# Four PSUM banks for attention scores: given out in fixed turn instead of by the pool's estimate (pre-norm attention with a routed expert layer, one core)

## The chip, the core and the metric

The kernel runs on one core of a Trainium2 chip. The metric is the device time of one execution in microseconds; lower is better. The kernel before the change was run three times: 604.11, 605.59 and 605.93 us, median 605.59. A profile was taken of one further execution. It took 598.14 us, of which 596.4 us lie between its first and its last instruction (the span).

## What is computed

One transformer layer in float32 on x of shape 8 x 512 x 128: attention on the normalised input, added back, and then a mixture of experts on the normalised sum, added back.

```
q = (x @ Wq).reshape(b, t, H, HD)            # H = 16 heads of HD = 8
k = (x @ Wk).reshape(b, t, H, HD)
v = (x @ Wv).reshape(b, t, H, HD)
s = jnp.einsum('bqhd,bkhd->bhqk', q * scale, k)
s = jnp.where(causal[None, None], s, -jnp.inf)
p = jax.nn.softmax(s, axis=-1)
o = jnp.einsum('bhqk,bkhd->bqhd', p, v).reshape(b, t, H * HD)
...
probs = jax.nn.softmax(logits / TEMPERATURE, axis=-1)       # 8 experts
topk_probs, topk_idx = jax.lax.top_k(probs, TOPK)           # the best 2
hidden = jax.nn.relu(jnp.einsum('th,ehf->tef', x_flat, w1) + b1[None])
all_out = jnp.einsum('tef,efh->teh', hidden, w2) + b2[None]
y_flat = jnp.sum(gathered * topk_probs[:, :, None], axis=1)
...
x = x + _L0_attn_ref(_layernorm(x, axis=-1), ...)
x = x + _L0_ffn_ref(_layernorm(x, axis=-1), ...)
```

## The kernel before

The work goes sequence by sequence: 8 sequences (b), each with 4 groups (g) of 4 heads. Several generators run side by side while the program is traced. Each yields a time of its own making, and a small loop at the end of the function always lets the one with the lowest time go on. What comes out is one written order for PE, ACT, DVE and SP, which these four engines keep (`ORDERED`, L1346 to L1359). POOL isn't in that set; its instructions are placed by the framework, apart from those that are pinned.

For each head the scores are computed twice. The generator `shifts` (L557) computes the scores with queries on the partitions, the tiles called s, for the row maximum alone: PE writes a bank of 128 x 512 float32 with up to four matmuls (L597, L602), and DVE reduces it to the maximum (pm, L616). When a group is done, the maxima are negated, split in two bfloat16 parts, turned by PE (nmTp, L562), copied by ACT (nmT, L564) and written by POOL's DMA as two more rows of the queries (L570). The generator `attend` (L642) then computes the scores with keys on the partitions, the tiles called st, with the shift by the row maximum already in the product: PE writes a bank (L752, L757) and ACT takes the exp of it into SBUF (pt, L762). PE multiplies the result with the values (po, L673). `shifts` runs some half a sequence ahead of `attend`, so that in the written order one unit of s tiles and one unit of st tiles take turns. A unit has two banks or one; in a group there are 10 s tiles and 10 st tiles.

All these tiles come from one pool of four PSUM banks, `ps_sc` (L123). A tile is asked for with `ps_sc.tile(..., tag="sc")` at L591 for s and at L747 for st. A third place asks for them too, after attention: the expert tiles ph of L1244, 42 of them, read by ACT and DVE (L1258, L1260) into hT. In all 682 tiles go through the four banks: 320 s, 320 st, 42 ph. Which of the four banks a tile gets is settled when the program is built: the framework estimates when each bank comes free, and gives the tile the one that it expects first. On the chip there is no choice left: the first matmul of the tile waits, by semaphore, for the reader of the tile that had the same bank before.

Three more banks (`ps_mm`, L124) serve all other products and transposes, and one (`ps_o`, L125) collects the output of attention. The expert layer runs in the generator `experts` (L1047): tiles of 128 tokens are gathered by expert, turned (xgTp, L1210), multiplied with w1 (ph, L1251), passed through bias and ReLU (hT), multiplied with w2 (py, L1110), given their second bias (yo, L1114) and scattered by POOL (ys, L1148). Part of it runs beside attention, the rest after it. Indirect transfers of POOL (L1016, L1148) are tied to the last exp that was written before them (`in_order`, L256). The generator `sums` adds the two choices of each token to x (L1329) and stores the result.

Of the kernel before, what the change touches and what calls it, by code (L numbers as in the profile page):

```python
# [9 lines left out]
F32 = mybir.dt.float32  # L10
# [5 lines left out]
PSUM = bass.MemoryType.PSUM  # L16
DRAM = bass.MemoryType.DRAM

P = 128
# [7 lines left out]
def preln_attn_moe(ctx: ExitStack, tc: tile.TileContext, x, wq, wk, wv, wo, bo,  # L27
# [37 lines left out]
    B, T, D = x.shape  # L65
    E, _, F = w1.shape
# [38 lines left out]
    for k, b in ((0, 1), (0, 3), (0, 5), (0, 6), (1, 7)):  # L105
        n = GROUPS[k].index(b) + 1
# [13 lines left out]
    work = ctx.enter_context(tc.tile_pool(name="work", bufs=2))  # L120
    small = ctx.enter_context(tc.tile_pool(name="small", bufs=2))
    slots = ctx.enter_context(tc.tile_pool(name="slots", bufs=1, space=DRAM))
    ps_sc = ctx.enter_context(tc.tile_pool(name="ps_sc", bufs=4, space=PSUM))  # L123
    ps_mm = ctx.enter_context(tc.tile_pool(name="ps_mm", bufs=3, space=PSUM))  # L124
    ps_o = ctx.enter_context(tc.tile_pool(name="ps_o", bufs=1, space=PSUM))  # L125

# [129 lines left out]
    def in_order(ins):  # L256
        tc.keep_in_program_order(ins)
        if last_exp[0] is not None:
            tc.add_manual_dep(
                ins.ins, last_exp[0].ins.name,  # L260
                mybir.DependencyInfo(
                    mybir.DependencyClass.Sync, mybir.DependencyReason.DATA
                ),
                reason="indirect transfers keep the pace of attention",
            )

    def mm_tile(name):
        return ps_mm.tile([P, T], F32, tag="mm", name=name)
# [14 lines left out]
    for k in range(2):  # L283
        n = E * ROOM[k] + SPARE * P
# [272 lines left out]
    def shifts():  # L557
        late = []

        def transposed(b, g, nh):  # L560
            pt = mm_tile(f"nmTp_{b}_{g}").bitcast(BF16)
            nc.tensor.transpose(pt[:, :P], nh, ident_bf)  # L562
            nmT = small.tile([32, P], BF16, tag="nmT", name=f"nmT_{b}_{g}")
            nc.scalar.copy(nmT, pt[:32, :P])  # L564
            late.append(lambda: rows(b, g, nmT))

        def rows(b, g, nmT):

            for l in range(2):
                ins = nc.gpsimd.dma_start(  # L570
                    out=q2_buf[b % 2][KS + l : KS + l + 1, HG * g : HG * g + HG],
                    in_=nmT[16 * l : 16 * l + 16],
                )
                if b > 0:
                    tc.keep_in_program_order(ins)
            shifted.add((b, g, 2))

        for b in range(B):
            for g in range(G):
                t0 = b - LEAD + g / G + (0.1 if b == 0 < g else 0.0)  # L580
                yield t0
                assert b in packed
                q2, k2 = q2_buf[b % 2], k2_buf[b % 2]

                pm = pm_buf[g % 2].rearrange("p (n u) t k -> p u n (t k)", u=2)
                for pr in range(2):
                    n = 2 * g + pr
                    for i, unit in enumerate(S_UNITS):
                        yield t0 + (3 * pr + i) / 24
                        for v, bank in enumerate(unit):  # L590
                            ps = ps_sc.tile(  # L591
                                [P, T], F32, tag="sc", name=f"s_{b}_{n}_{i}_{v}"
                            )
                            for u, t, at in bank:
                                h, q = 2 * n + u, ts(t, P)
                                if t > 0:
                                    nc.tensor.matmul(  # L597
                                        ps[:, at : at + t * P], lhsT=q2[:KS, h, q],
                                        rhs=k2[:KS, h, : t * P],
                                        start=(at == 0), stop=True, skip_group_check=True,  # L600
                                    )
                                nc.tensor.matmul(  # L602
                                    ps[:, at + t * P : at + (t + 1) * P],
                                    lhsT=q2[:, h, q], rhs=k2[:, h, q],
                                    start=(at + t == 0), stop=True, skip_group_check=True,
                                )
                            blocks = ps.rearrange("p (a q) -> p a q", q=P)
                            if i == 0:
                                top, src = pm[:, v, pr, 12:13], ps
                            elif i == 1:  # L610
                                top, src = pm[:, v, pr, 3:7], blocks
                            else:
                                top, src = pm[:, :, pr, 8], ps.rearrange(
                                    "p (u k) -> p u k", u=2
                                )
                            nc.vector.tensor_reduce(top, src, AX.X, ALU.max)  # L616
                        if t0 + (3 * pr + i) / 24 < 0:
                            keep_warm(WARM[2], f"{g}_{pr}_{i}")
                        if late:
                            late.pop(0)()  # L620
                nm = small.tile([P, HG * NT], F32, tag="nm", name=f"nm_{b}_{g}")
                nc.vector.tensor_reduce(
                    nm, pm_buf[g % 2].rearrange("p h t k -> p (h t) k"), AX.X, ALU.max,
                    negate=True,
                )
                nh = nh_buf[g % 2]
                nm = nm.rearrange("p (h o a) -> p h o a", o=2, a=2)
                hi, lo = (
                    nh[:, ts(l, HG * NT)].rearrange("p (h a o) -> p h o a", a=2, o=2)
                    for l in range(2)  # L630
                )
                V.tensor_copy(hi, nm)
                V.tensor_tensor(lo, nm, hi, ALU.subtract)
                if b > 0:
                    late.append(lambda: None)
                late.append(lambda b=b, g=g, nh=nh: transposed(b, g, nh))
        while late:
            late.pop(0)()
            yield B - LEAD + 0.05


    def attend():  # L642
# [90 lines left out]
        for b in range(B):  # L733
            for g in range(G):
                yield b + g / G
                assert (b, g, 2) in shifted
                q2, k2 = q2_buf[b % 2], k2_buf[b % 2]
                for i, unit in enumerate(T_UNITS):
                    pts = []
                    for pr in range(2):  # L740
                        yield b + g / G + (2 * i + pr + 0.5) / 24
                        n = 2 * g + pr
                        pt = work.tile(
                            [P, 2, T], F32, tag="pt", name=f"pt_{b}_{n}_{i}", bufs=6
                        )
                        for v, bank in enumerate(unit):
                            ps = ps_sc.tile(  # L747
                                [P, T], F32, tag="sc", name=f"st_{b}_{n}_{i}_{v}"
                            )
                            for u, j, at in bank:  # L750
                                h, k = 2 * n + u, ts(j, P)
                                nc.tensor.matmul(  # L752
                                    ps[:, at : at + P], lhsT=k2[:, h, k], rhs=q2[:, h, k],
                                    start=(at == 0), stop=True, skip_group_check=True,
                                )
                                if j < NT - 1:
                                    nc.tensor.matmul(  # L757
                                        ps[:, at + P : at + T - j * P],
                                        lhsT=k2[:KO, h, k], rhs=q2[:KO, h, (j + 1) * P :],
                                        start=False, stop=True, skip_group_check=True,  # L760
                                    )
                            last_exp[0] = nc.scalar.activation(pt[:, v, :], ps, AF.Exp, scale=SCALE)  # L762
                        pts.append(pt)
                        go_on()
                    products.append(lambda b=b, g=g, pts=pts, unit=unit, i=i: product(
                        b, g, pts, unit, i == 0, i == 2))
                attended.add((b, g))
# [279 lines left out]
    def experts():  # L1047
# [192 lines left out]
        for n, (s, i) in enumerate(tiles):  # L1240
            first, m = quad(s, i)
            yield when(s, i + 1)
            if after(s, i):
                ph = ps_sc.tile([P, T], F32, tag="sc", name=f"ph_{s}_{i}")  # L1244
                hT = work.tile([P, 2, T], F32, tag="pt", name=f"hT_{s}_{i}", bufs=6)
                hT = hT[:, 0, :].rearrange("p (c t) -> p c t", c=FC)
            else:
                ph = mm_tile(f"ph_{s}_{i}")
                hT = work.tile([P, FC, P], F32, tag="hT", name=f"hT_{s}_{i}")
# [138 lines left out]
```

## Time and profile before

| | before |
|---|---|
| median of three runs | 605.59 us |
| profiled execution | 598.14 us |
| its span | 596.4 us |
| mean granted TensorE clock | 0.954 |
| PE matmul rows of the s tiles, first to last start | 25.7 to 428.7 us |
| PE matmul rows of the st tiles, first to last start | 44.9 to 462.5 us |
| exp of st (L762), 320 | 179.1 us busy, 600 ns mean |
| maximum of s (L616), 320 | 206.0 us busy, 682 ns mean |
| idle time of ACT before the exps | 128.1 us |
| idle time of DVE before the maxima | 36.4 us |

Engines are PE (matmul), PEld (its weight loads), DVE, ACT, POOL and SP. "L762 ACT ACTIVATE pt<-st" is line 762, an instruction of ACT that writes the tile pt and reads the tile st. A line such as "PE s L597 <- ACT pt L762: 12.8, 23, 2.4" in the list of waits says that PE's matmuls into s at line 597 were held up, with the engine idle, until an instruction of ACT at line 762 had ended: 12.8 us in total, 23 times, at most 2.4 us. A PE row's end is modelled, since matmuls overlap in the array.

### The profile page before, as it was taken

How to read it: one execution, taken by the hardware profiler on the slowest of the kernel's cores; microseconds unless marked ns; L12 is line 12 of the kernel's file. 1: busy time of each engine (PE TensorE's matmuls, PEld its weight loads, DVE VectorE, ACT ScalarE, POOL GpSimd, SP SyncE). 2: the span in 40 equal slices, each digit the busy share in tenths (PEclk: the TensorE clock that was granted, in tenths of full speed). 3: DMA queues.
4: the chain of work that ended last, by engine and by line, in shares of the span. 5: the costliest groups of instructions: out<-in, count | busy, mean ns of one | idle time of the engine just before them, and what ended most of it. 6: DMA issues, size and time to landing. Idle time of an engine off the chain costs nothing. (4 is left out here: it accounts for less than half of the span.)

```text
span 596.4 us, 14010 instructions
## 1 busy us (share of the span) xinstructions
PE 515.4 (86%) x4762; PEld 378.0 (63%) x4762; DVE 430.9 (72%) x1367; ACT 306.5 (51%) x673; POOL 220.2 (37%) x278
## 2 busy tenths in 40 slices
PE   6979999988888988888799999998899788879980
PEld 4745455545445565665566777766576687879970
DVE  7788778898778977978788877797753354323694
ACT  2646656665645566465447465654454233345530
POOL 4032202315514422533443336335335334654441
PEclk9888899999979999999799999999999788999995
DMA  2568198188199455406502784322344586668783
GB/s 57 160 133 186 28 226 210 38 214 215 27 208 181 125 142 127 124 19 179 149 30 67 180 202 120 89 64 73 87 116 114 181 248 185 192 184 246 243 293 110
DMA packets 68762, 86.07 MB, mean 144 GB/s; under 512 B 11540, under 2 KB 50748, under 8 KB 66652
## 3 DMA queue, kind: packets, MB, share of 16 engines
q1 hardware_dynamic: 61508, 74.87, 49.1%
q0 software_dynamic: 6592, 9.65, 5.0%
q8 instruction: 39, 0.64, 0.5%
q10 hardware_dynamic: 592, 0.66, 0.4%
q14 instruction: 31, 0.25, 0.2%
HBM read 61.34 MB, written 26.16 MB: 147 GB/s over the span
## 5 line engine op out<-in xcount | busy, mean ns | idle before, releaser
L762 ACT ACTIVATE pt<-st 128x512 f32<-128x512 f32 x320 | 179.1, 600 | 128.1 <-PE st L752 58.3
L616 DVE TENSOR_REDUCE pm<-s 128x1 f32<-128x512 f32 (+2 forms) x320 | 206.0, 682 | 36.4 <-PE s L602 30.3
L1148 POOL DMA_INDIRECT ys<-yo,to x78 | 76.1, 975 | 125.4 <-ACT pt L762 50.2
L597 PE MATMUL s<-k,q 72*128 72x384 bf16 (+2 forms) x384 | 93.9, 280 | 16.0 <-ACT pt L762 12.8
L752 PE MATMUL st<-q,k 128*128 128x128 bf16 x512 | 92.9, 222 | 14.8 <-ACT pt L762 6.4
L602 PE MATMUL s<-k,q 128*128 128x128 bf16 x512 | 94.3, 223 | 7.4 <-ACT pt L762 5.5
L757 PE MATMUL st<-q,k 74*128 74x256 bf16 (+2 forms) x384 | 93.9, 280 | 0.0
L673 PE MATMUL po<-pt,va 128*18 128x512 f32 (+3 forms) x1024 | 92.5, 445 | 0.5 <-ACT pt L762 0.3
L1110 PE MATMUL py<-w_sb,hT 128*128 x624 | 88.6, 286 | 4.2 <-DVE yo L1114 2.0
L1016 POOL DMA_INDIRECT xs<-xn_f,slot x64 | 63.2, 987 | 64.1 <-ACT pt L762 35.7
L1110 PEld LDWEIGHTS py<-w_sb,hT 128*128 128x128 f32 x624 | 79.5, 199 | 8.2 <-issue 3.6
L602 PEld LDWEIGHTS <-q 128*128 128x128 bf16 x512 | 51.0, 100 | 37.7 <-issue 34.8
L570 POOL DMA_DIRECT2D q<-nmT x64 | 33.7, 529 | 76.4 <-ACT nmT L564 71.1
L597 PEld LDWEIGHTS <-q 72*128 72x128 bf16 x384 | 37.8, 100 | 36.5 <-issue 29.7
L752 PEld LDWEIGHTS <-k 128*128 128x128 bf16 x512 | 51.6, 101 | 6.3 <-issue 2.4
L757 PEld LDWEIGHTS <-k 74*128 74x128 bf16 x384 | 37.7, 98 | 26.2 <-issue 20.8
L673 PEld LDWEIGHTS po<-pt,va 128*18 128x18 f32 x1024 | 23.1, 97 | 29.6 <-issue 22.7
L1251 PE MATMUL ph<-xgT,wt 128*128 128x128 f32 x288 | 41.0, 286 | 0.8 <-ACT pt L762 0.8
L1251 PEld LDWEIGHTS ph<-xgT,wt 128*128 128x128 f32 x288 | 35.8, 195 | 5.7 <-issue 2.4
L1258 ACT ACTIVATE hT<-ph,q 128x128 f32<-128x128 f32 x72 | 21.0, 368 | 27.9 <-PE ph L1251 11.7
L1258 ACT ACTIVATE hT<-ph,wt 128x128 f32<-128x128 f32 x72 | 20.6, 367 | 22.3 <-issue 10.9
L456 POOL TENSOR_TENSOR part<-rest,part 128x512 bf16<-128x512 f32 x14 | 16.2, 1162 | 41.6 <-issue 33.8
(172 smaller groups left out, 688.0 us busy)
## 6 DMA issues: line engine op xcount, KB each, us to landing
wt<-wrows SPq DMA_DIRECT2D x36, 322.0 KB
k<-kparts SPq DMA_DIRECT2D x42, 192.0 KB
q<-wrows SPq DMA_DIRECT2D x24, 322.0 KB
k<-wrows SPq DMA_DIRECT2D x18, 322.0 KB
q<-qparts SPq DMA_DIRECT2D x30, 192.0 KB
q<-ys SPq DMA_DIRECT2D x15, 256.0 KB
k<-xs SPq DMA_DIRECT2D x42, 65.0 KB
qparts<-part SPq DMA_DIRECT2D x14, 192.0 KB
```

The costliest lines, as they stand in the source:

```text
L597: nc.tensor.matmul(ps[:, at : at + t * P], lhsT=q2[:KS, h, q], rhs=k2[:KS, h, : t * P], start=(at == 0), stop=True, skip_group_check=True,)
L602: nc.tensor.matmul(ps[:, at + t * P : at + (t + 1) * P], lhsT=q2[:, h, q], rhs=k2[:, h, q], start=(at + t == 0), stop=True, skip_group_che ...
L616: nc.vector.tensor_reduce(top, src, AX.X, ALU.max)
L673: nc.tensor.matmul(po[32 * h : 32 * h + 2 * VC, j * P :], lhsT=va[:, j, c0 : c0 + 2 * VC], rhs=at_cols(pts[pr], unit, u, at, W), start=(fi ...
L752: nc.tensor.matmul(ps[:, at : at + P], lhsT=k2[:, h, k], rhs=q2[:, h, k], start=(at == 0), stop=True, skip_group_check=True,)
L757: nc.tensor.matmul(ps[:, at + P : at + T - j * P], lhsT=k2[:KO, h, k], rhs=q2[:KO, h, (j + 1) * P :], start=False, stop=True, skip_group_c ...
L762: last_exp[0] = nc.scalar.activation(pt[:, v, :], ps, AF.Exp, scale=SCALE)
L1016: ins = nc.gpsimd.indirect_dma_start(out=xs[k], out_offset=bass.IndirectOffsetOnAxis(ap=slot[b][:, j * NT + i : j * NT + i + 1], axis=0), ...
L1110: nc.tensor.matmul(py, lhsT=hT[:, c, :], rhs=w2_sb[:, bass.ds(at[s, i] + c * E * D, D)], start=(c == 0), stop=(c == FC - 1),)
L1148: ins = nc.gpsimd.indirect_dma_start(out=ys[k], out_offset=bass.IndirectOffsetOnAxis(ap=to[s, first][:, i - first : i - first + 1], axis=0 ...
L1251: nc.tensor.matmul(ph[:, ts(c, P)], lhsT=wt[s, i][:, ts(c, P)], rhs=turned[s, first][:, ts(i - first, P)], start=True, stop=True,)
L1258: nc.scalar.activation(hT[:, c, :], ph[:, ts(c, P)], AF.Relu, bias=bias)
```

## The change

The pool `ps_sc` gets four tags of one buffer each in place of one tag of four buffers. A counter in the new function `score_tile` walks over the four tags; all three places that asked the pool for a tile now ask `score_tile`. So the bank of a tile is that of the tile four before it in traced order. The number of banks, the instructions and the written order of PE, ACT, DVE and SP stay.

```
-    ps_sc = ctx.enter_context(tc.tile_pool(name="ps_sc", bufs=4, space=PSUM))
+    ps_sc = ctx.enter_context(tc.tile_pool(name="ps_sc", bufs=1, space=PSUM))
...
+    turn = [0]
+
+    def score_tile(name):
+        turn[0] = (turn[0] + 1) % 4
+        return ps_sc.tile([P, T], F32, tag=f"sc{turn[0]}", name=name)
...
-                            ps = ps_sc.tile(
-                                [P, T], F32, tag="sc", name=f"s_{b}_{n}_{i}_{v}"
-                            )
+                            ps = score_tile(f"s_{b}_{n}_{i}_{v}")
...
-                            ps = ps_sc.tile(
-                                [P, T], F32, tag="sc", name=f"st_{b}_{n}_{i}_{v}"
-                            )
+                            ps = score_tile(f"st_{b}_{n}_{i}_{v}")
...
-                ph = ps_sc.tile([P, T], F32, tag="sc", name=f"ph_{s}_{i}")
+                ph = score_tile(f"ph_{s}_{i}")
```

## The prediction

> **What bounds the kernel now.** I read the page's busy times first, then the chain of waits, the list of who waited for whom, the view of the tiles s and st, and last the timeline, stretch by stretch.
>
> ```profile
> span 596.4 us, 14010 instructions
> ...
> PE 515.4 (86%) x4762; PEld 378.0 (63%) x4762; DVE 430.9 (72%) x1367; ACT 306.5 (51%) x673; POOL 220.2 (37%) x278
> ```
>
> PE is the busiest engine, DVE second. The chain that ended last, by line:
>
> ```profile
> PE py L1110 7%; PE ph L1251 6%; DVE x L1329 1%; PE xgTp L1210 1%; DMA q<-ys 1%; ACT hT L1258 0%; DVE yo L1114 0%; DVE hT L1260 0%; DMA ys<-yo,to 0%; PE pp L725 0%; PE oqp L694 0%; PE oTp L717 0%; ACT xgT L1212 0%; PE pl L801 0%; POOL ys L1148 0%
> ```
>
> What carries time there are PE's expert matmuls after attention; attention ends with the last exp at 463 us, and from there a late PE is a late end. So what PE loses in attention is lost at the end.
>
> The list of waits shows what a full pool costs PE today:
>
> ```profile
> PE s L597 <- ACT pt L762: 12.8, 23, 2.4
> ...
> PE st L752 <- ACT pt L762: 6.4, 12, 1.0
> ...
> PE s L602 <- ACT pt L762: 5.5, 9, 1.6
> ...
> PE st L752 <- DVE pm L616: 3.3, 7, 1.0
> ```
>
> Columns: total us, times, longest. A matmul that opens a score tile waits for the reader of the bank's last tile, and that reader is mostly an exp. The reader of the other kind, the row maximum, is slower:
>
> ```profile
> L616 DVE TENSOR_REDUCE pm<-s x320: 656/680/694, 26.1 to 429.5; 128x1 f32<-128x512 f32 x64, 128x4 f32<-128x512 f32 x64, 128x2 f32<-128x512 f32 x32
> ```
>
> The exp's row has 570/597/656 ns. The gap in durations is small; the gap in queueing isn't. I put the 682 tiles of the pool in PE's order, gave each the bank that the compiled program of before has for it, its first matmul's start, and its reader's end. An s tile holds its bank 1.90 us on average from first matmul to release, an st tile 1.33; a reduce begins a median 0.61 us after its scores stand, an exp 0.17. The shortest time from a release to the next tile's first matmul is 0.050 us.
>
> **The change part by part.** It adds no instruction and removes none; PE, ACT, DVE and SP keep their written order. It changes which reader a tile's first matmul waits for: always that of the tile four before. Today that holds for 265 of the 678 tiles that follow another; 413 reuse a bank 1, 2, 3, 5, 6 or 7 tiles old. The first 31 tiles and all 42 ph tiles (L1251) have distance four already; the closest ph tile finds its bank free 3.1 us before it, so they cost nothing.
>
> *What it removes.* 81 tiles start after a gap of over 0.1 us that a bank's release ended, 33.9 us in all: 28.0 behind an exp, 5.9 behind a reduce. At 75 tiles that wait for their bank at distance other than four, the bank four back was free sooner; the part of the gap that goes is 14.1 us.
>
> *What it adds.* For 80 tiles, the reader four back ended later than the tile began: 37.5 us, of which 36.7 behind reduces. Neither sum is the price, because PE is one queue: once late, it finds the following banks free. One stretch shows it:
>
> ```profile
> 250.00 0.32 PE L597 MATMUL s<-k,q 72*128 72x384 bf16 x1 [0.43 <-ACT pt L762]
> ...
> 250.49 0.22 PE L752 MATMUL st<-q,k 128*128 128x128 bf16 x1
> ...
> 250.56 0.66 DVE L616 TENSOR_REDUCE pm<-s 128x2 f32<-128x512 f32 x1
> ...
> 251.62 0.22 PE L752 MATMUL st<-q,k 128*128 128x128 bf16 x1 [0.74 <-ACT pt L762]
> ```
>
> The s tile at 250.00 took the bank of the exp that ended at 249.95. In turn, its bank is that of the reduce that ends at 250.56 + 0.66 = 251.22: it begins at 251.27, 1.27 us late. The st tile after it follows by PE's own 0.39 (the first tile's matmuls end at 250.39), at 251.66. The next st tile waits today until 251.62 for the exp of the tile just before it (distance one); in turn its bank was free at 250.44, so it follows at 252.05. Loss 1.27, left after two tiles: 0.43. Behind the waiting matmul stand, in PE's order, the st tiles, products (L673) and expert matmuls; ACT waits for st (58.3 + 57.1 us of its idle time), and POOL's indirect transfers for the exps (50.2 + 35.7 us). POOL is busy 37%, so I cost that at nothing; without that cover, the 1.27 would stand in the transfers too.
>
> *The sum.* Four ways, in growing order of merging. Nothing merges: +37.5 − 14.1 = +23.4. Tiles at most 2 apart count once, by their largest: 24.9 − 13.1 = +11.8. At most 10 apart: 14.3 − 8.4 = +5.9. And the walk of the stretch above carried through all tiles, with PE's spacing, every reader's own duration and the other waits as the rows have them: PE is late by 1.2 us at 100, 2.0 at 143, 2.9 at 219, 3.9 at 274, 3.1 at 361, and +3.8 remain at the end. The same walk with today's banks ends 1.9 us short of the trace, so half of that is the method's error. I take **+4.5**, nearer to the walk, as it alone lets a delay be made up at a later wait for something else. With all reduces 7% longer the walk gives +7.2, with them 7% shorter −0.5; with no bank limit at all −6.7, the floor for any order.
>
> *Bounds on what the trace can't show.* Waits that don't fit an instruction are extra instructions on PE; 66 stand before L597 and L752. If as many came or went at 0.05 each: ±3.3; I take 0, since one wait replaces one. The other pools still choose by estimates, which will move; I have no row for that and let the range hold it.
>
> *The clock.* Windows of the trace, before and after two slow stretches (columns: window, busy us of PE, PEld, DVE, ACT, POOL, then granted clock, DMA share, GB/s):
>
> ```profile
> 165.60:172.40 6.80, 4.78 (x54) 2.58 (x54) 6.32 (x24) 3.51 (x7) 1.00 (x2) 1.00 1.07 237
> 172.40:179.20 6.80, 6.80 (x44) 3.57 (x42) 4.98 (x14) 2.47 (x5) 0.00 (x0) 0.50 0.90 192
> 285.00:291.80 6.80, 4.74 (x52) 3.12 (x52) 4.79 (x21) 2.28 (x7) 3.95 (x4) 1.00 0.45 116
> 291.80:298.70 6.90, 5.77 (x30) 3.88 (x33) 4.65 (x13) 3.73 (x9) 2.11 (x3) 0.51 0.78 209
> ```
>
> After 6.8 us with PE 70% busy the clock is halved for about 6.8 us. At half rate such a stretch costs some 3.4 us. But 100 to 150 us has 16 bank gaps (5.85 us) and the full clock throughout, so gaps of this size alone don't do it. I take 0 and keep +6.8 (two more stretches) as upper end. The Trainium skill speaks against the change here: "TensorE: Matmul & The Clock Gate", section "A second HAM failure mode: psum-queue depth-cycling", says that matmul groups cycling through PSUM banks with short idle times between can make the clock swing between half and full. By the rule alone the sum would be +4.5 + 6.8 or more; by the row of 100 to 150 it stays +4.5.
>
> The profiled execution took 598.14 us (span 596.4); the median of the runs shown is 605.59, 1.2% above. I add the microseconds to the median unscaled: 605.6 + 4.5 = **610.1**.
>
> **The rivals.**
> A. *Faster: the strict turn ends the reuse of a bank just taken.* Place: 100 to 300 us, where most exp-bound gaps lie. For it: 28.0 of the 33.9 us are behind exps, and choices at distance one or two are plainly bad ones. Against it: DVE, 72% busy, holds banks longest, and strict turn ties st tiles to it. Price: if later waits swallow half of the losses by group of twenty tiles (17.1 / 2) while the gains at most 4 apart stay (11.6), −3.0: 602.6. It decides if reduces start sooner than in this trace, by some 7%.
> B. *No change: the waits only swap.* Gains and losses within 1.8 us; that the pool's turn comes out as it was belongs here too, though 413 other distances leave it 1 in 100. 605.6.
> C. *Slower by more: new waits halve the clock.* At 425 us two s tiles would begin 1.6 and 2.0 us late, near 169 us one 1.3. If two more stretches like 172.40 follow, +4.5 + 6.8: 616.9.
>
> **How the numbers follow.** Forecast 0.58 (its own range +2 to +9: 607.6 to 614.6), A 0.15, B 0.15, C 0.12. No change means within 0.3%, 1.8 us, about what a measurement of this kernel can tell: faster 0.15, same 0.15, slower 0.58 + 0.12 = 0.70. For 8 in 10 I cut half of A below and most of C above: 602.8 to 615.6.
>
> **What would show it.** In the list of waits, PE s and PE st behind ACT pt fall from about 28 us to under 15, behind DVE pm rise from some 6 to over 25. The idle time of ACT before pt behind PE st grows past 115 us. PE's last score matmul, at 462.5 us now, comes 3 to 5 us later, and the stretch from there to the end keeps its 134 us. The forecast is wrong if bank waits behind reduces stay under 15 us, if the delay is made up in the tail, or if the number of half-clock stretches differs.

## The result, and the profile after

The changed kernel took 610.05 us (median of 20 runs, 603.95 to 614.30), the kernel before 604.29 us (20 runs, 597.99 to 609.09) in the same comparison. The ratio is 1.0138, 95% interval 1.0107 to 1.0168: slower. The ratio leaves out runs that took over 1.5% more than the fastest of their kernel; over all runs the medians are 5.8 us (0.95%) apart. The forecast was 610.1 us and slower, by 4.5 us.

In the two compiled programs the instructions of each engine are the same and in the same order, POOL's too, and of all tile addresses only those of 474 score tiles differ. So whatever differs beyond the spread between executions comes from the banks.

From the page of the changed kernel, the span, the busy times and the two lines of the chain that ended last (the lines of the source have moved by 2 to 6: 620 is the maximum, 764 the exp):

```profile
span 608.5 us, 14010 instructions
...
PE 521.8 (86%) x4762; PEld 380.5 (63%) x4762; DVE 429.5 (71%) x1367; ACT 304.2 (50%) x673; POOL 220.0 (36%) x278
...
PE 50%; DVE 26%; issue 10%; DMA 5%; ACT 5%; POOL 2%; DVEq 0%; POOLq 0%; ACTq 0%
DVE pm L620 11%; PE po L677 10%; PE py L1112 9%; PE ph L1253 9%; PE st L759 4%; PE s L601 4%; PE st L754 3%; DMA q<-nmT 3%; PE s L606 3%; ACT pt L764 3%; DVE x L1331 2%; DVE hT L1262 2%; PE pq L452 2%; PE oqp L698 2%; ACT hT L1260 1%
```

The chain can be followed further back here than before, where it broke off at 463 us, so the shares aren't to be compared one by one; but it runs through PE and DVE in turn, with the maxima alone at 11% of the span. The list of waits of the changed kernel (total us, times, longest):

```profile
ACT pt L764 <- PE st L759: 60.9, 68, 5.4
ACT pt L764 <- PE st L754: 60.4, 42, 3.5
...
PE s L601 <- DVE pm L620: 15.5, 19, 2.0
...
PE s L606 <- DVE pm L620: 7.9, 15, 1.6
...
PE st L754 <- DMA q<-nmT: 5.6, 3, 3.5
...
PE st L754 <- DVE pm L620: 4.2, 22, 0.3
...
PE st L754 <- ACT pt L764: 1.4, 4, 0.4
```

The waits behind exps, 24.7 us in three lines of the list before, are down to 1.4; those behind maxima are up to 27.6. By the tile list of the prediction (gaps over 0.1 us that a bank's release ended) it is 28.0 behind exps and 5.9 behind reduces before, 2.3 and 32.8 after. The kind has changed and the sum hardly: 33.9 and 35.1 us. The pair of profiles from one chip, further below, has more between them: 30.3 and 33.9.

The stretch that the prediction walked through lies some 10 us later here. PE's rows of the timeline, then DVE's:

```profile
257.59 0.33 PE L601 MATMUL s<-k,q 72*128 72x384 bf16 x1
257.75 0.22 PE L606 MATMUL s<-k,q 128*128 128x128 bf16 x1
259.72 0.48 PE L601 MATMUL s<-k,q 72*128 72x384 bf16 x1 [1.74 <-DVE pm L620]
259.99 0.31 PE L606 MATMUL s<-k,q 128*128 128x128 bf16 x1
260.10 0.31 PE L754 MATMUL st<-q,k 128*128 128x128 bf16 x1
```

```profile
257.31 1.11 DVE L1262 TENSOR_SCALAR hT<-ph,wt 128x128 f32<-128x128 f32 x4
258.33 0.34 DVE L377 TENSOR_SCALAR xn_a<-x,mv_a,rstd_a 128x128 f32<-128x128 f32 x1
258.58 0.29 DVE L362 BATCH_NORM_STATS2 stats_f<-x 128x6 f32<-128x128 f32 x1
258.91 0.18 DVE L363 BATCH_NORM_AGGREGATE mv_f<-stats_f 128x2 f32<-128x6 f32 x1
259.01 0.66 DVE L620 TENSOR_REDUCE pm<-s 128x2 f32<-128x512 f32 x1
```

PE stands 1.74 us because the bank in turn is that of a tile whose maximum waits on DVE behind seven other instructions. Two exps ended within this time (at 258.44 and 258.93); their banks were free and not allowed. Not every such wait is of this kind: of 51 waits of over 0.1 us in which an s tile waited for an earlier s tile's maximum, 28 had another of the four banks free sooner, by 13.0 of 27.9 us in all; in the other 23 no bank was.

One pair of profiles can mislead. Their spans are 12.1 us apart, and from the first to the last matmul of an st tile 17.1 us (417.5 and 434.6). Much of that isn't the banks: the trace's clock records have 20.5 us at half clock in this stretch before, and 41.0 after, which by the price worked out below (0.31 to 0.38 us for each) is 6.4 to 7.8 us. The bank gaps have 1.2 us more, PE's other gaps of over 0.1 us 4.9 us more (5.2 and 10.1); where the rest lies the pair doesn't show. The experiments separate clock and banks.

### The profile page after: what moved, and what is told of

It is laid out like the page before. It is cut to its first block, busy times and chain, and to the rows that moved or that the text cites. A ratio compares the mean times of both kernels' runs of the same rounds, so it can differ in the third digit from the quotient of the medians.

```text
span 608.5 us, 14010 instructions
## 1 busy us (share of the span) xinstructions
PE 521.8 (86%) x4762; PEld 380.5 (63%) x4762; DVE 429.5 (71%) x1367; ACT 304.2 (50%) x673; POOL 220.0 (36%) x278
## 4 chain that ended last, share of the span: by engine, by line
PE 50%; DVE 26%; issue 10%; DMA 5%; ACT 5%; POOL 2%; DVEq 0%; POOLq 0%; ACTq 0%
DVE pm L620 11%; PE po L677 10%; PE py L1112 9%; PE ph L1253 9%; PE st L759 4%; PE s L601 4%; PE st L754 3%; DMA q<-nmT 3%; PE s L606 3%; ACT pt L764 3%; DVE x L1331 2%; DVE hT L1262 2%; PE pq L452 2%; PE oqp L698 2%; ACT hT L1260 1%
## 5 line engine op out<-in xcount | busy, mean ns | idle before, releaser
L764 ACT ACTIVATE pt<-st 128x512 f32<-128x512 f32 x320 | 177.2, 599 | 140.8 <-PE st L759 60.9
L601 PE MATMUL s<-k,q 72*128 72x384 bf16 (+2 forms) x384 | 96.0, 284 | 22.6 <-DVE pm L620 15.5
L606 PE MATMUL s<-k,q 128*128 128x128 bf16 x512 | 96.4, 226 | 9.8 <-DVE pm L620 7.9
L677 PE MATMUL po<-pt,va 128*18 128x512 f32 (+3 forms) x1024 | 99.7, 460 | 2.5 <-ACT pt L764 2.5
L677 PEld LDWEIGHTS po<-pt,va 128*18 128x18 f32 x1024 | 23.7, 98 | 36.1 <-issue 24.7
L462 POOL TENSOR_TENSOR part<-rest,part 128x512 bf16<-128x512 f32 x14 | 16.2, 1161 | 40.9 <-issue 34.6
```

The lines of the kernel that those rows point to most:

```text
L601: nc.tensor.matmul(ps[:, at : at + t * P], lhsT=q2[:KS, h, q], rhs=k2[:KS, h, : t * P], start=(at == 0), stop=True, skip_group_check=True,)
L606: nc.tensor.matmul(ps[:, at + t * P : at + (t + 1) * P], lhsT=q2[:, h, q], rhs=k2[:, h, q], start=(at + t == 0), stop=True, skip_group_che ...
L677: nc.tensor.matmul(po[32 * h : 32 * h + 2 * VC, j * P :], lhsT=va[:, j, c0 : c0 + 2 * VC], rhs=at_cols(pts[pr], unit, u, at, W), start=(fi ...
```

## The experiments

Two theories. **D**: strict turn makes PE wait for late maxima, and this is the loss. **K**: the loss is the halved clock. The kernels of all twelve runs keep the order of PE, ACT, DVE and SP. POOL's order is that of before too, except in turn5 (two places) and in the two with a shorter maximum (six places, alike in both).

The numbers in one table. Gaps are those of the tile list, in us, behind exps and behind reduces. The last column comes from all runs of one chip, a straight line of time over mean granted clock with one slope for the chip and a constant for each kernel: the difference of the constants to before, with its standard error. It is blank for the change, since the clocks of before's runs in that comparison are not on record.

| kernel | ratio to before, 95% interval | gaps | at equal clock, us |
|---|---|---|---|
| the change | 1.0138, 1.0107 to 1.0168 | 2.3 + 32.8 | |
| t_before | 1.0037, 0.9994 to 1.0080 | 28.4 + 6.3 | +1.6 ± 0.7 |
| half1 | 1.0105, 1.0039 to 1.0171 | 16.1 + 18.1 | +3.8 ± 0.9 |
| half2 | 1.0069, 1.0025 to 1.0112 | 13.3 + 20.5 | +0.2 ± 0.7 |
| split22 | 1.0107, 1.0049 to 1.0165 | 6.7 + 37.5 | +7.0 ± 0.9 |
| t_measured | 0.9871, 0.9822 to 0.9921 | 11.5 + 12.2 | −5.9 ± 0.7 |
| short_before | 0.9779, 0.9721 to 0.9838 | 28.9 + 1.0 | −7.6 ± 0.8 |
| short_after | 0.9679, 0.9628 to 0.9730 | 4.4 + 11.7 | −17.3 ± 0.7 |
| turn_again | 1.0072, 1.0021 to 1.0123 | 2.0 + 32.8 | +5.0 ± 0.7 |
| t_before_2 | 1.0002, 0.9961 to 1.0044 | 23.2 + 7.2 | −0.3 ± 0.7 |
| turn_3 | 1.0107, 1.0045 to 1.0169 | 2.1 + 31.8 | +5.3 ± 0.9 |
| turn5 | 1.0240, 1.0195 to 1.0284 | 1.3 + 21.4 | +11.9 ± 0.9 |
| t_measured_2 | 0.9917, 0.9878 to 0.9956 | 11.5 + 12.1 | −5.4 ± 0.7 |

**The program of before, from a table.** A table names the tag of each of the 682 tiles; with the choices of before, each tile follows the same tile in its bank as before.

```
-    turn = [0]
+    turn = [-1]
+    BANKS = (
...
     def score_tile(name):
-        turn[0] = (turn[0] + 1) % 4
-        return ps_sc.tile([P, T], F32, tag=f"sc{turn[0]}", name=name)
+        turn[0] += 1
+        return ps_sc.tile([P, T], F32, tag=f"sc{BANKS[turn[0]]}", name=name)
```

> Banks read from a table that repeats the choices of before; every instruction and every reuse of a bank is that of before. Both theories: ratio 1.000 to before within 0.003; if the four tags themselves cost anything, it is slower. Its profile is a second look at before: theory D (DVE's late release of banks is the loss) expects bank gaps of PE of about 34 us again, 28 behind exps; theory K (the halved clock is the loss) expects its half-clock time in attention near 17 us again, as in the first profile of before, and not near 37 us as in that of the change.

> The program of before once more from the table, as the other half of a pair of profiles on one chip with turn_3. Ratio 1.000 to before, within 0.004. PE's bank gaps about 34 us, 28 of them behind exps.

Ratios 1.0037 and 1.0002: the tags cost nothing that shows, and the +1.6 and −0.3 us say how far an equal-clock number of the others may be trusted. The gaps come back, 34.7 and 30.3 us. The half-clock time between first and last st tile does not: 34.1 and 27.3 us where the first profile of before had 20.5 (the expectation counted from 50 to 450 us, which gives 17 for before and 37 for the change). So the 41.0 of the changed kernel's first profile proves nothing about the banks; in the same program it moves by 14 us between executions.

**The change again.** No edit.

> The changed kernel once more, beside the others on one chip. Ratio 1.011 to 1.017 to before. Theory D: a second profile shows some 33 us of bank gaps behind reduces again and under 5 behind exps. Theory K: half-clock time in attention over 30 us again, and at equal granted clock the runs are no longer than those of before.

> The changed kernel a third time. Theory D with a loss of about 5 us at equal granted clock, as in turn_again: ratio 1.007 to 1.010, and a line of time over granted clock that runs 4 to 6 us above that of before. Theory K: no distance between the two lines.

1.0072 and 1.0107. The first lies under its range, with an interval that reaches into it, the second just over its own. The half-clock time between first and last st tile is 20.5 and 27.3 us, not over 30 as K had it, and the bank gaps behind reduces are 32.8 and 31.8 us, as D had it. At equal clock the changed kernel is 5.0 and 5.3 us longer, the distance that D expects and K doesn't. And its mean clock isn't lower than that of before: 0.9662 against 0.9624 on the one chip, 0.9617 against 0.9624 on the other. In the pair of profiles from one chip, t_before_2 and turn_3, both have 27.3 us at half clock between first and last st tile. That stretch takes 415.0 and 419.1 us, and the bank gaps are 30.3 and 33.9. So 3.6 of the 4.1 us stand in the gaps themselves; where the rest lies these profiles don't settle.

**Only half of the sequence.** The table of before, with strict turn up to tile 319 (half1) or from there on (half2).

```
+    BANKS = strict[:319] + before[319:]      # half1
+    BANKS = before[:319] + strict[319:]      # half2
```

(Short for the 682 digits that stand in each kernel.)

> Strict turn for the first 319 tiles (up to sequence 4 of the scores), the choices of before from there. Theory D, with the walk of the prediction: +2.9 of its +3.8 us come before 219 us, so three quarters of the whole loss: ratio 1.010 if the whole is 1.0138. A loss spread evenly over the tiles gives 1.007. Theory K: no fixed share; it follows the half-clock time of the run.

> The choices of before for the first 319 tiles, strict turn from there. Theory D by the walk: a quarter of the loss, ratio 1.003. Evenly spread: 1.007. The two halves together should give the whole, 1.0138, in theory D; in theory K they need not add.

1.0105 and 1.0069, with intervals that overlap; at equal clock 3.8 and 0.2 us, so there the first half costs more, as the walk has it. Half2 is above the 1.003, though its interval holds it; its runs had a mean clock of 0.9452 against 0.9492. At equal clock the halves add up to 4.0 us, beside 5.0 and 5.3 for the whole on other chips. With the 1.6 us by which the same program from a table was off on this chip, "more in the first half" is what can be said, not "three quarters".

**Two banks for each reader.**

```
...
+        kind = ("s", "st", "ph").index(name.split("_")[0])
+        turn[kind] += 1
+        bank = turn[kind] % 4 if kind == 2 else 2 * kind + turn[kind] % 2
...
```

> Two banks for s in turn and two for st in turn, four in turn for ph. An st tile never waits for a reduce, an s tile never for an exp. If tying st to DVE's reduces were the loss (a simple reading of theory D), this is not slower than before: ratio 0.995 to 1.0. If the loss comes from a fixed order with too few banks for the slower reader, s tiles wait more than before and the ratio is 1.005 to 1.02, with PE's gaps behind reduces over 30 us and behind exps under 10.

1.0107, the second branch. From its list of waits:

```profile
PE s L603 <- DVE pm L622: 17.4, 24, 1.6
PE s L608 <- DVE pm L622: 17.2, 44, 1.6
PE st L756 <- ACT pt L766: 6.1, 11, 2.3
```

No st tile can wait for a maximum here, and it is as slow as strict turn. So the loss doesn't need ACT's tiles to be tied to DVE's; s tiles that wait for earlier s tiles are enough. Strict turn is nearer to this kernel than it looks: since units of s and st mostly take turns two by two, the tile four back of an s tile is an s tile 199 times in 316. That a free bank stood by while an s tile waited is shown for part of the waits of the changed kernel above, not for this one.

**Early maxima.** Half of the columns are left out of the row maximum, which takes a reduce from 0.68 to 0.42 us; once with the choices of before, once with strict turn.

```
-    top, src = pm[:, v, pr, 12:13], ps
+    top, src = pm[:, v, pr, 12:13], ps[:, : T // 2]
...
-    top, src = pm[:, v, pr, 3:7], blocks
+    top, src = pm[:, v, pr, 3:7], blocks[:, :, : P // 2]
...
     "p (u k) -> p u k", u=2
-    )
+    )[:, :, : P]
```

> The choices of before, and the row maximum taken over half of each row's columns (half of the columns are left out of the maximum), so that a reduce takes about 0.35 instead of 0.68 us and DVE has some 105 us less to do. Both theories: faster than before by 1 to 2%, since reduces queue less; PE's gaps behind exps stay near 28 us, since the choices stay.

> Strict turn, and the row maximum over half of the columns, as in short_before. Theory D: with early reduces strict turn loses nothing; it is as fast as short_before or up to 1% faster, and PE's gaps behind reduces fall from 33 us to under 15. Theory K, or a cost of strict turn that does not come from DVE: still 1.0 to 1.5% slower than short_before.

The reduce shrank less than was expected (0.42 for 0.35 us), and the times fell by a little more than was forecast. What counts is the pair: 0.9779 and 0.9679. With early maxima strict turn is 1.0% **faster**, 9.7 us at equal clock; the sign has turned. Waits of short_before, then of short_after:

```profile
PE s L612 <- ACT pt L775: 11.6, 26, 0.7
PE st L765 <- ACT pt L775: 11.0, 24, 1.0
PE s L617 <- ACT pt L775: 4.9, 10, 0.5
```

```profile
PE s L601 <- DVE pm L620: 7.2, 12, 0.8
...
PE s L606 <- DVE pm L620: 4.3, 7, 2.4
...
PE st L754 <- ACT pt L764: 2.9, 7, 0.7
```

The choices of before still reuse banks that an exp has only just taken, 27.5 us in these lines. Strict turn is rid of these waits as in the full kernel, and the new ones behind maxima are small, 11.5 us. Gaps and time move together: by the table the gaps of strict turn are 13.8 us fewer with the short maximum, and 3.6 us more with the full one (the pair from one chip), and the times at equal clock are 9.7 us less and 5.0 to 5.3 us more. A shorter reduce also gives DVE some 80 us less to do (105 had been expected), so this pair doesn't tell a reduce's own length from its place in DVE's queue.

**A table from measured durations.** The tiles are gone through in PE's order; each gets the bank whose reader ends first when the rows of the trace of before are carried forward as in the walk. 357 of the tiles come out at distance four.

```
-    BANKS = before
+    BANKS = measured
```

(Short for the digits, as above.)

> A table that gives each tile the bank whose reader ends first by the durations of the trace of before. Theory D: fewer waits than before, some 2.4 us less by the walk, ratio 0.996, and 1.8% under strict turn; PE's bank gaps under 25 us. Theory K: ratio 1.00 to before, unless its half-clock time falls too.

> The table from the measured durations once more, on this chip. Ratio 0.984 to 0.992 to before; bank gaps of PE about 24 us. If its gain on the other chip was that chip's, the ratio is over 0.995.

0.9871 on one chip and 0.9917 on another: the best of the kernels that do the whole work, better than both. Its list of waits from the first run:

```profile
PE st L765 <- DVE pm L631: 6.3, 16, 1.5
...
PE s L612 <- ACT pt L775: 6.2, 16, 0.7
...
PE s L617 <- ACT pt L775: 2.9, 6, 0.5
```

Gaps fall to 23.6 us and are shared by both readers. The gain, 5.9 and 5.4 us at equal clock, is over twice what the walk gave (2.4), and near the 6.7 that it gave for no bank limit at all, though 23.6 us of gaps are left. So the walk may put waits at too little.

**Five banks in turn.**

```
-    ps_mm = ctx.enter_context(tc.tile_pool(name="ps_mm", bufs=3, space=PSUM))
+    ps_mm = ctx.enter_context(tc.tile_pool(name="ps_mm", bufs=2, space=PSUM))
...
-        turn[0] = (turn[0] + 1) % 4
+        turn[0] = (turn[0] + 1) % 5
```

> Five banks for the scores in strict turn, two instead of three for the other products. Theory D: an st tile is tied to a reduce five tiles back instead of four, which has nearly always begun; by the walk some 8 us less than four in turn, ratio 0.990 to 0.998 to before, with bank gaps of the score tiles under 25 us. If the third bank of the other products is needed, that gain is eaten up and the ratio is over 1.005.

1.0240, the slowest of all. The gaps of the score tiles are down to 22.7 us, as D has it, now nearly all of them st tiles behind maxima, and PE waits more elsewhere:

```profile
ACT pt L764 <- PE st L759: 77.1, 65, 5.4
...
PE st L754 <- DVE pm L620: 19.5, 41, 2.1
...
PE py L1112 <- ACT hT L1260: 3.3, 4, 1.3
...
PE pv L547 <- DVE rest L458: 3.1, 1, 3.1
...
PE xnTp_f L391 <- DVE rest L458: 1.3, 1, 1.3
```

The instruction rest reads a tile of ps_mm that neither pv nor xnTp_f needs, so in those two lines PE waited for a bank of the smaller pool; of py's wait for hT the list doesn't tell. PE's gaps of over 0.1 us between first and last st tile that aren't bank gaps of score tiles are 16.2 us, against 3.2 in t_before_2 on the same chip. That the missing bank is behind all of this isn't shown: POOL's order differs too, in two places.

## Why the prediction was right, and where it was off

*Direction and mechanism: right, and shown.* The step "of which 36.7 behind reduces" named the maxima as what the change waits for. The list of waits has it, and with shorter maxima the same change of banks turns the sign (short_before and short_after). The walk had said that the sign depends on the reduces' length by some 7%; at 39% shorter the gain is 1.0%.

*Size: right within the noise of the clock.* Forecast +4.5; 5.0 and 5.3 at equal clock on two chips, 5.8 by the medians of the first comparison. Its ratio gives 8.3. The walk's own +3.8 was a little low; of the four ways to add up, the two that merge most (+3.8, +5.9) hold the measured value, and +11.8 and +23.4 are out. That late tiles share one delay was the step that mattered. That +4.5 came within a microsecond holds some luck: the same walk was 1.9 us off with the banks of before, and 3 us short for the measured table. Of its inputs one is miscounted: of some 75 tiles that wait for their bank at another distance than four, the bank four back was free sooner for 47, not for all; the 14.1 us stand.

*What it removes: right.* In the list of waits those behind exps fell to 1.4 us (forecast: under 15), those behind reduces rose to 27.6 (over 25). ACT's idle time before pt behind PE st rose from 115.4 to 121.3 us (past 115), but this sign tells little: in the pair from one chip it is 125.8 and 127.2.

*The single stretch: right.* The s tile at 250.00 was to come 1.27 us later; with the 0.43 us that it waited already, that is 1.70 us of idle time, and the profile has 1.74. The two late tiles forecast at 425 us (1.6 and 2.0 in today's rows) came as 1.59 and then 0.21 us of idle time: the second finds most of its delay already paid by the first. The one near 169 us (1.3) came as 1.25.

*Why strict turn loses: half wrong.* Against rival A the prediction had set that "strict turn ties st tiles to it", to DVE. That is not the main thing: of the 27.6 us behind maxima 23.4 are s tiles behind earlier s tiles, and split22, where no st tile is tied to a maximum, loses as much.

*No cost for the other pools and POOL: right*, and by more than was known: the compiled programs agree in all of it. The extra wait instructions, taken at 0, are 66 before the score matmuls in both traces.

*"3 to 5 us later, and the stretch from there to the end keeps its 134 us": wrong.* The last score matmul came 17.1 us later and the rest took 129.1 us. What failed is reading one profile against one profile: the half-clock time moved by 20 us at the one place and the other way at the other. In the pair from one chip it is 4.6 us later (459.4 and 464.0), and the rest takes 118.0 and 116.4 us. So two of the prediction's three signs of being wrong (a delay made up in the tail, another number of half-clock stretches) did come up in the first pair. They can't decide, because one program's own half-clock time moves by 14 us.

*The clock: taken at 0, right; its price was too high.* I put a half-clock stretch of 6.8 us at 3.4, half its length. The lines of time over clock have 3.7 to 4.6 us for 0.01 of mean clock, and 0.01 of some 580 to 600 us stands for 12 us at half clock, so one such us costs 0.31 to 0.38. Rival C doesn't hold: the change doesn't lower the mean clock. The Trainium skill's "TensorE: Matmul & The Clock Gate", section "A second HAM failure mode: psum-queue depth-cycling", would have short waits between groups make the clock swing; here more maxima-bound waits and fewer exp-bound ones left it where it was (0.9617 and 0.9624). As the sum of the gaps hardly changed, that is no test of the section itself.

*Rival B* would have been the verdict from the sum of gaps alone (33.9 and 35.1 us). It isn't, since the medians and both equal-clock numbers are over its bound of 1.8 us.

## What to carry to other kernels

When two readers of different speed share a set of banks, a fixed turn makes the writer wait for the later one; whether that beats a compile-time estimate depends on how late the slow reader ends: its wait in its engine's queue (a median of 0.61 us here, against 0.17 of the fast one) and its duration, which the short maximum cut. Lay each tile's first write beside the end of its bank's last reader: the list gives the waits of any other assignment, if delays on one engine are merged and not added, and a table made from it beat both rules here. Before comparing two profiles, compare their granted clock.

## What was not expected of the hardware

The kernel before took 604.29 us (median) in the first comparison; on the three chips of the experiments it took 601.23, 574.95 and 575.32 us. Of the 26.8 us between the spans of t_before and t_before_2, 15.8 lie after attention, in the same instructions. Windows from the last st tile to the end, t_before and then t_before_2 (window, busy us of PE, PEld, DVE, ACT, POOL, granted clock, DMA share, GB/s):

```profile
470.20:604.10 133.90, 102.06 (x833) 97.47 (x832) 64.42 (x280) 47.44 (x151) 57.76 (x60) 0.92 0.68 209
```

```profile
459.20:577.30 118.10, 97.27 (x833) 93.97 (x831) 63.55 (x277) 48.05 (x150) 57.68 (x60) 0.94 0.78 238
```

DMA moved 209 GB/s there on the one and 238 on the other; the clock differs by 0.02. What makes one chip faster wasn't tried. The ratios above are each within one chip.
